# Last rows of a two-layer graph kernel: one-hot products and a sync-engine store in place of a GpSimd scatter

## The chip, the core and the metric

The kernel runs on one core of a Trainium2 chip. A core has TensorE (PE, matrix products), VectorE (DVE), ScalarE (ACT), GpSimd (POOL) and SyncE (SP), each with an instruction queue of its own; they meet through semaphores. Transfers are issued from a queue (SP's, ACT's or GpSimd's) and carried out by 16 DMA engines. The metric is the device time of one execution in microseconds (us), as the median of several runs.

## The reference

A graph of 6,250 nodes with 256 features and 106,250 edges sorted by destination (each node's last edge is its loop to itself), two layers. Cut to what matters:

```
S    = x[src]                                     # layer 0: a small net on each edge, by its type
msgs = where(rel == r, relu(relu(S @ W_r.T + b_r) @ W_r.T + b_r), msgs)      # r = 0, 1
agg  = segment_sum(msgs, dst)
x1   = layernorm(x + mlp(lstm_cell(agg)))

h    = x1 @ W                                     # layer 1: attention with 4 heads
e    = leaky_relu(a_src[src] + a_dst[dst])
ex   = exp(e - segment_max(e, dst)[dst])
y    = segment_sum(h[src] * ex, dst) / segment_sum(ex, dst) + bias + x1
out  = layernorm(x1 + relu(layernorm(y) * gamma + beta))                      # 6250 x 256, float32
```

Layer 1 in the kernel has the loop edges taken out of the list and added on their own.

## The kernel before

**Stages.** The front (gnn_kernel) computes layer 0's message rows for all nodes and both edge types on TensorE (`fph` L1228, `fpm` L1242, addition of the bias into `fms` on VectorE L1250, relu on ScalarE L1253, store to `parts` by SP L1255), while VectorE packs the edge list, GpSimd moves it by 21 indirect transfers (L944), and VectorE unpacks it into index tables. It ends with a flag `odd_i` (L1120 to L1125): if it is 0 all engines branch (L1281) into `fast`, else into a general kernel. The front's order is the planner's, helped by a few dependencies written by hand; `fast` runs under a manual schedule: each queue holds its instructions in the order in which the program emits them.

**Windows and groups.** The 100,000 list edges are 782 tiles of 128. Seven tiles are a window (NW = 112), and a window touches at most 64 consecutive destination rows, from `low[w]` on, a number that is known only on the chip. Two windows are a group (NG = 56): its 128 partitions are the 64 rows of its first window and the 64 of its second. For each tile GpSimd gathers 128 source rows (L1367, `G`), and TensorE adds them up with a one-hot matrix of slots (layer 0: L1777; layer 1: L2101, after VectorE's weighting in `weighted`, L1992).

**Layer 1.** At its start `complete` mends tiles that were gathered before the last rows of layer 0 were stored: VectorE builds one-hot matrices `ohS` from the loaded `srcb` and from `own_n` (L1853), TensorE multiplies (L1859). `own_n[p, q]` is the node that partition p of the q-th of the last LATE = 3 groups owns, or -1. When a group's sum is complete, `finish(g)` makes its 128 rows in the ring buffer `fy` (three of them): VectorE and ScalarE alternate, and the last step is ScalarE's normalisation (L2047). The rows of both windows are then stored by SP, each with 64 rows at `low[w]` (L2058). Neighbouring windows' stores overlap, so each waits until the one before it has landed. The windows of the last group are excepted (`lows_of` stops at NW - 2), because 64 rows from their start would go past the end of the result: group NG - 1 is scattered row by row by GpSimd, to the indices `tail_i` (L2060, where rows past the end are dropped). After it come the branch at the end of `fast` and, on every engine, the program's closing instructions (L2210).

Of the kernel before, what the change touches and what calls it, by code (L numbers as in the profile page):

```python
# [33 lines left out]
F32 = mybir.dt.float32  # L34
I32 = mybir.dt.int32
AF = mybir.ActivationFunctionType
OP = mybir.AluOpType
# [5 lines left out]
P = 128  # L43
N = 6250
D = 256
E = 106250
H = 4
# [20 lines left out]
NW = -(-TC // WT)  # L68
SLOTS = 64
NG = NW // 2  # L70
# [9 lines left out]
LATE = 3  # L80
# [627 lines left out]
def gnn_kernel(  # L708
# [26 lines left out]
    nc = tc.nc  # L735
# [4 lines left out]
    def rows(ap, n):  # L740
# [13 lines left out]
    iota_f = const.tile([P, P], F32, name="fiota")  # L754
    nc.gpsimd.iota(
        iota_f, pattern=[[1, P]], base=0, channel_multiplier=0, allow_small_or_imprecise_dtypes=True
# [16 lines left out]
    tail_i = const.tile([P, 1], I32, name="tail_i")  # L773
    tail_x = const.tile([P, 1], I32, name="tail_x")
    idx_e = const.tile([P, EARLY], I32, name="idx_e")
    own_n = const.tile([P, LATE], F32, name="own_n")


    with (
# [18 lines left out]
        with (  # L798
# [89 lines left out]
            moved = lp.tile([P, NC, HB + P], I32, name="moved")  # L888
# [53 lines left out]
            for k in range(NC):  # L942
                for b in range(3):
                    move = nc.gpsimd.indirect_dma_start(  # L944
                        out=packed,
                        out_offset=bass.IndirectOffsetOnAxis(ap=place[:CT, b, k : k + 1], axis=0),
                        in_=frame[:CT, k, b * HB : (b + 1) * HB],
                        in_offset=None,
# [62 lines left out]
            low = lp.tile([1, NW + 1], F32, name="low")  # L1011
            nc.vector.tensor_scalar(low, low_r, 1.0, None, op0=OP.add)
            nc.vector.memset(low[:, 0:1], 0.0)
            nc.vector.memset(low[:, NW:], float(N + 1))
            nc.vector.tensor_copy(low_i, low)
            wide = lp.tile([1, NW + 1], F32, name="wide")
            nc.vector.tensor_sub(wide[:, :NW], low[:, 1:], low[:, :NW])
            nc.vector.tensor_scalar(wide[:, :NW], wide[:, :NW], float(SLOTS), None, op0=OP.is_gt)
            nc.vector.tensor_scalar(
                wide[:, NW : NW + 1], low[:, NW - 3 : NW - 2], float(N - SLOTS), None, op0=OP.is_gt  # L1020
            )
            odd = lp.tile([1, 8], F32, name="odd")
            nc.vector.tensor_reduce(odd[:, 5:6], wide, axis=AX.X, op=OP.add)

            list_i = both[:CT, 0, :, :]
# [64 lines left out]
            for to, of in (  # L1090
# [31 lines left out]
            nc.vector.tensor_scalar(odd[:, 4:5], odd[:, 4:5], float(CT * NC - TC), None, op0=OP.subtract)  # L1122
            nc.vector.tensor_scalar(odd[:, 0:6], odd[:, 0:6], 0.0, None, op0=OP.not_equal)
            nc.vector.tensor_reduce(odd[:, 6:7], odd[:, 0:6], axis=AX.X, op=OP.add)
            nc.vector.tensor_scalar(odd_i, odd[:, 6:7], 1.0, None, op0=OP.min)  # L1125

            low_p = lps.tile([P, NW + 1], F32, name="low_p", bufs=1)
# [29 lines left out]
                op0=OP.is_ge,  # L1157
# [13 lines left out]
            for half, first_w, next_w in ((lo, w0, w0 + 1), (hi, w0 + 1, w0 + 2)):  # L1171
# [6 lines left out]
                    op0=OP.add,  # L1178
# [38 lines left out]
        for b0, bn in [(0, 1)] + [(1 + b, n) for b, n in blocks_of(NB - 1, CHUNK)]:  # L1217
# [6 lines left out]
            for r in range(2):  # L1224
                for m in range(2):
                    ph = mps.tile([P, CHUNK * P], F32, name="fph")
                    for k in range(2):
# [4 lines left out]
                            start=(k == 0),  # L1232
                            stop=(k == 1),
# [4 lines left out]
            for j in range(bn):  # L1238
                pm = mps.tile([P, 2, D], F32, name="fpm")
                for r in range(2):  # L1240
                    for k in range(2):
# [4 lines left out]
                            start=(k == 0),  # L1246
                            stop=(k == 1),
# [33 lines left out]
    with tc.If(odd_v == 0) as cmp:  # L1281
        fast(
            tc, x, WihT, bih, bhh, W1T, b1, W2T, b2, W3T, b3, Wg, att_src, att_dst, bias, gamma,
            beta, out, parts0, rows1, slots, cuts, kept, iota_f, iota_p, ident, idx0, idx1,
            first, mark, slot, low_i, tail_i, tail_x, idx_e, own_n, srcs,
        )
# [8 lines left out]
def fast(  # L1295
# [40 lines left out]
    nc = tc.nc  # L1336
# [12 lines left out]
    def windows_of(g):  # L1349
        return range(2 * g, 2 * g + 2)  # L1350

    def lows_of(ws):

        ws = [w for w in ws if w < NW - 2]
        return dict(zip(ws, lows(ws[0], len(ws)))) if ws else {}
# [18 lines left out]
    class Steps:  # L1374
# [18 lines left out]
        def finish(self):  # L1393
            while self.chains:
                self.step()

    def half_of(w):
        return slice(SLOTS * (w % 2), SLOTS * (w % 2 + 1))
# [42 lines left out]
    def ring(pool, shape, dtype, name, n):  # L1441

        of = rings.setdefault((name, id(pool)), [[], 0])
        if len(of[0]) < n:
            of[0].append(pool.tile(shape, dtype, name=f"{name}_{len(of[0])}"))
        of[1] += 1
        return of[0][(of[1] - 1) % n]
# [11 lines left out]
    def in_order(done, g):  # L1459
        if g != len(done):  # L1460
            raise ValueError("groups are out of order")
        done.append(g)
# [4 lines left out]
    with (  # L1467
# [320 lines left out]
        for n in range(TC + LAG):  # L1788
            if n < TC:
                g, t = order[n]  # L1790
# [21 lines left out]
            if n >= LAG:  # L1812
                g, t = order[n - LAG]
# [13 lines left out]
    with (  # L1827
# [171 lines left out]
        def finish(g, ps):  # L1999
            ws = windows_of(g)  # L2000
            u = everyone
            n = u.stop
            at_w = lows_of(ws)
            k3 = k3s[g]
            sm = ring(fp, [P, 4, H], F32, "sm", 3)
            w_own, den = sm[u, 0, :], sm[u, 1, :]
            nc.vector.tensor_sub(w_own, loop[u, g, :], ps[u, HA:])

            nc.vector.tensor_scalar(w_own, w_own, 0.0, None, op0=OP.min)
            nc.scalar.activation(w_own, w_own, AF.Exp)  # L2010
            yield 2

            nc.vector.tensor_scalar(w_own, w_own, 2.0, None, op0=OP.mult)
            nc.vector.scalar_tensor_tensor(
                den, ps[u, D:HA], 1e-16, w_own, op0=OP.add, op1=OP.add
            )
            nc.vector.reciprocal(den, den)
            yt = ring(fp, [P, D], F32, "fy", 3)
            y = yt[u, :]

            def heads(ap):
                return ap.rearrange("p (h f) -> p h f", h=H)

            nc.vector.tensor_mul(  # L2024
                heads(y), heads(k3[u, 2, :]), w_own[:, :, None].to_broadcast([n, H, F])
            )
            nc.vector.tensor_add(y, y, ps[u, :D])  # L2027
            read.add(g)
            yield 1
            nc.vector.tensor_mul(heads(y), heads(y), den[:, :, None].to_broadcast([n, H, F]))  # L2030
            nc.vector.tensor_add(y, y, k3[u, 1, :])  # L2031
            yield 1
            mv = ring(fp, [P, 2, 2], F32, "fmv1", 3)
            rs = ring(fp, [P, 2, 2], F32, "frs1", 3)

            def normed(k):
                st = ring(fp, [P, nc.vector.BN_STATS_DIM], F32, "fst1", 3)
                r, m = rs[u, k, 0:1], rs[u, k, 1:2]
                nc.vector.bn_stats(st[u, :], y)  # L2039
                nc.vector.bn_aggr(mv[u, k, :], st[u, :])  # L2040
                nc.scalar.activation(r, mv[u, k, 1:2], AF.Ln, bias=eps_c[u])  # L2041
                nc.scalar.activation(r, r, AF.Exp, scale=-0.5)
                yield 2
                nc.vector.scalar_tensor_tensor(  # L2044
                    m, mv[u, k, 0:1], -1.0, r, op0=OP.mult, op1=OP.mult
                )
                nc.scalar.activation(y, y, AF.Identity, bias=m, scale=r)  # L2047

            yield from normed(0)
            yield 2  # L2050
            nc.vector.tensor_mul(y, y, vec_p[u, 0, :])
            nc.vector.tensor_add(y, y, vec_p[u, 1, :])
            nc.vector.scalar_tensor_tensor(y, y, 0.0, k3[u, 0, :], op0=OP.max, op1=OP.add)
            yield 1
            yield from normed(1)
            in_order(written, g)
            for w in at_w:
                nc.sync.dma_start(out[bass.ds(at_w[w], SLOTS), :], yt[half_of(w), :])  # L2058
            if g == NG - 1:
                nc.gpsimd.indirect_dma_start(  # L2060
                    out=out,
                    out_offset=bass.IndirectOffsetOnAxis(ap=tail_i, axis=0),
                    in_=yt,
                    in_offset=None,
                    bounds_check=N - 1,
                    oob_is_err=False,
                )

        pair_of = {g: p for p in pairs for g in p}
        boxes = {p[0]: {} for p in pairs}  # L2070
        sums, queue, read, ohs, k3s, left, written = {}, [], set(), {}, {}, {}, []

        def sum1():

# [27 lines left out]
            if left[g] == 0:  # L2102
                run.start(finish(g, sums[g]), 1)

        def aheads():
            for pair in pairs:
                while run.now < 2 * WT * (pair[0] - (len(pair) == 1)):
                    yield 1
                yield from ahead(pair, boxes[pair[0]])

        run.start(aheads())
        t = 0
        while t < TC + LAG or late or queue or run.chains:
# [8 lines left out]
            if 0 <= k < TC:  # L2122
# [3 lines left out]
                g = w // 2  # L2126
# [87 lines left out]
```

## Time and profile before

| what | value |
|---|---|
| median of 3 runs | 2231.43 us (2231.18 to 2232.48) |
| the profiled execution | 2231.32 us, its span 2229.5 us, mean granted TensorE clock 0.829 |
| busy in the span | PE 1576.9, DVE 1259.0, ACT 506.4, POOL 1527.2 us |
| GpSimd gathers, both layers | 782 of 957 ns and 761 of 956 ns |
| first gather of layer 0, last gather of layer 1 | start at 196.91 us and 2177.11 us |
| last ScalarE instruction of group NG - 1 | 2216.27 us, 0.60 us long |
| the scatter of the last rows | 2217.15 us, 1.00 us long on GpSimd |

The span runs from the first to the last instruction on record. Busy time of GpSimd is the time in which it makes descriptors; the transfers themselves follow on the DMA engines. An engine's name with a q (SPq, POOLq) means its instruction sequencer: branches, waits and issues are recorded there and do not count as busy. In rows of a view by line, three durations are the minimum, median and maximum in ns.

### The profile page before, as it was taken

What the parts mean: (1) busy time and instruction counts of PE and PEld (TensorE: products, weight loads), DVE (VectorE), ACT (ScalarE), POOL (GpSimd) and SP (SyncE); (2) the same over time, 40 slices, a digit from 0 to 9 for tenths busy, and PEclk for the clock granted to TensorE, in tenths of its full rate; (3) what the DMA queues carried; (4) which work ended last, traced back from release to release, by engine and by line L of the source; (5) the groups of instructions that cost most, each with busy time, mean ns of one, the idle gap of its engine ahead of it and who ended that gap; (6) DMA issues with size and microseconds to landing.
All of it is one profiled execution on the core that took longest, in us unless ns stands there. A gap on an engine that the chain in (4) does not pass through costs nothing. (4 is left out here: it accounts for less than half of the span.)

```text
span 2229.5 us, 22334 instructions
## 1 busy us (share of the span) xinstructions
PE 1576.9 (71%) x5848; PEld 789.2 (35%) x5848; DVE 1259.0 (56%) x3374; ACT 506.4 (23%) x1526; POOL 1527.2 (68%) x1604
## 2 busy tenths in 40 slices
PE   8997788888888888888996754654545545454563
PEld 5664233333333333333453522322322223232331
DVE  7562134334333333333543688887777777777785
ACT  3332012221222212222343022212112111212121
POOL 1303777777777777777776777777777777777770
PEclk9998799899999899999997967766767677676776
DMA  5335435555455555554565556556555555555551
GB/s 165 131 103 155 130 114 172 165 153 149 147 171 165 146 151 155 170 168 134 178 175 162 150 145 165 156 145 165 148 153 156 144 159 143 164 155 145 156 151 38
DMA packets 163982, 334.33 MB, mean 150 GB/s; under 512 B 42538, under 2 KB 74398, under 8 KB 163845
## 3 DMA queue, kind: packets, MB, share of 16 engines
q0 software_dynamic: 75968, 208.00, 34.3%
q1 hardware_dynamic: 86085, 121.77, 17.3%
q10 hardware_dynamic: 1792, 3.05, 0.5%
q8 instruction: 48, 0.79, 0.1%
q14 instruction: 89, 0.73, 0.1%
HBM read 280.16 MB, written 52.53 MB: 149 GB/s over the span
## 5 line engine op out<-in xcount | busy, mean ns | idle before, releaser
L1367 POOL DMA_INDIRECT G<-parts,fidx x782 | 748.3, 957 | 330.5 <-issue 218.4
L1367 POOL DMA_INDIRECT G<-rows,fidx x761 | 727.4, 956 | 231.8 <-issue 214.2
L1777 PE MATMUL fps<-G,oh 128*64 128x257 f32 (+1 forms) x1674 | 528.1, 428 | 146.3 <-DMA G<-parts,fidx 129.5
L2101 PE MATMUL fps<-gw,oh 128*64 128x264 f32 (+1 forms) x1674 | 433.7, 463 | 246.3 <-DVE gw L1992 246.1
L2101 PEld LDWEIGHTS fps<-gw,oh 128*64 128x64 f32 (+1 forms) x1674 | 222.7, 164 | 411.9 <-DVE gw L1992 266.0
L1777 PEld LDWEIGHTS fps<-G,oh 128*64 128x64 f32 (+1 forms) x1674 | 193.6, 148 | 454.7 <-DMA G<-parts,fidx 237.2
L1992 DVE TENSOR_TENSOR gw<-G,bank 128x1792 f32<-128x1792 f32 (+1 forms) x167 | 248.9, 1490 | 62.4 <-ACT gw L1991 60.4
L1545 DVE TENSOR_SCALAR kind<-fps 128x1 f32<-128x1 f32 x112 | 12.5, 153 | 315.0 <-PE fps L1777 315.0
L1627 PE MATMUL fpg<-faT,fWihT 128*128 128x512 f32 (+2 forms) x432 | 170.9, 519 | 0.2 <-DVE faT L1563 0.2
L1452 DVE TENSOR_TENSOR oh<-bank,fslot 128x1024 f32<-128x1024 f32 x112 | 136.1, 1215 | 7.2 <-ACT bank L1971 7.2
L1940 PE MATMUL turn<-fident,e 128*120 128x128 f32 (+2 forms) x30 | 12.3, 412 | 155.3 <-ACT e L2136 155.3
L1242 PE MATMUL fpm<-fWrT,fhT 128*128 128x256 f32 x392 | 92.9, 392 | 5.3 <-DVE fms L1250 5.3
L1627 PEld LDWEIGHTS fpg<-faT,fWihT 128*128 128x128 f32 x432 | 70.9, 190 | 69.1 <-issue 59.4
L1738 DVE COPY nd<-hr 128x4 f32<-128x4 f32 x53 | 10.1, 190 | 149.7 <-ACT hr L1716 149.7
L1228 PE MATMUL fph<-fxc,fWrT 128*128 128x512 f32 (+1 forms) x208 | 88.8, 579 | 4.7 <-DMA fWrT<-in_WrT_dram 4.7
L2047 ACT ACTIVATE fy<-fy,frs 128x256 f32<-128x256 f32 x112 | 66.8, 596 | 86.9 <-DVE frs L2044 39.4
L2041 ACT ACTIVATE frs<-fmv,eps_c 128x1 f32<-128x1 f32 x112 | 32.9, 294 | 235.7 <-DVE gw L1986 152.7
L1242 PEld LDWEIGHTS fpm<-fWrT,fhT 128*128 128x128 f32 x392 | 75.6, 196 | 24.3 <-DVE fms L1250 9.1
L1710 PE MATMUL fpg<-Wx,fyT 128*128 128x264 f32 x224 | 74.2, 460 | 3.0 <-ACT fyT L1701 3.0
L944 POOL DMA_INDIRECT packed<-frame,place x21 | 20.9, 995 | 76.7 <-DVE frame L909 70.6
L1250 DVE TENSOR_TENSOR fms<-fpm,fbrr 128x512 f32<-128x512 f32 x49 | 33.6, 688 | 68.7 <-PE fpm L1242 62.8
L2144 ACT COPY e<-G 128x28 f32<-128x28 f32 x112 | 23.8, 213 | 183.8 <-DMA G<-rows,fidx 147.2
(253 smaller groups left out, 1863.4 us busy)
## 6 DMA issues: line engine op xcount, KB each, us to landing
kept<-keep SPq DMA_DIRECT2D x56, 384.0 KB
k<-kept SPq DMA_DIRECT2D x56, 384.0 KB
dB<-slots SPq DMA_DIRECT2D x112, 128.0 KB
loop<-parts SPq DMA_DIRECT2D x110, 128.0 KB
parts<-fms SPq DMA_DIRECT2D x49, 256.0 KB
G<-parts,fidx POOLq DMA_INDIRECT x782
G<-rows,fidx POOLq DMA_INDIRECT x761
fxn<-in_x_dram SPq DMA_DIRECT2D x110, 64.0 KB
```

What stands on the lines that cost most here:

```text
L1228: nc.tensor.matmul(ph[:, :cols], WrT_s[:, r, k, m * P : (m + 1) * P], xc[:, k, :cols], start=(k == 0), stop=(k == 1),)
L1242: made = nc.tensor.matmul(pm[:, r, :], hT[:, r, k, j * P : (j + 1) * P], WrT_s[:, r, k, :], start=(k == 0), stop=(k == 1),)
L1250: nc.vector.tensor_add(ms.rearrange("p r f -> p (r f)"), pm.rearrange("p r f -> p (r f)"), brr)
L1367: return nc.gpsimd.indirect_dma_start(out=to_tile, out_offset=None, in_=table, in_offset=bass.IndirectOffsetOnAxis(ap=idx, axis=0),)
L1452: nc.vector.tensor_tensor(to[:, :nj, :], iota_s[:, None, :].to_broadcast([P, nj, SLOTS]), of[:, :, None].to_broadcast([P, nj, SLOTS]), op= ...
L1627: nc.tensor.matmul(pg[:, :cols], WihT_s[:, k, c * P : (c + 1) * P], aT[:, k, :cols], start=(k == 0), stop=(k == 1),)
L1710: nc.tensor.matmul(ph[u, :], hs[i][:, k, u], Wx[:, k, :], start=(k == 0), stop=(k == 1))
L1777: nc.tensor.matmul(sums[g][to, :], ohj, got[t], start=begins, stop=ends)
L1992: nc.vector.tensor_mul(gw[:, :, :D].rearrange("p j (h f) -> p j h f", h=H), of[:, :n, :D].rearrange("p j (h f) -> p j h f", h=H), ex[:, o ...
L2041: nc.scalar.activation(r, mv[u, k, 1:2], AF.Ln, bias=eps_c[u])
L2047: nc.scalar.activation(y, y, AF.Identity, bias=m, scale=r)
L2101: nc.tensor.matmul(sums[g][to, :], ohj, gw, start=begins, stop=ends)
```

## The change

The last 128 rows of the result, 6122 to 6249, always lie in the last two groups if window NW - 4 begins at row 6122 or before. The changed kernel checks that on the chip (`odd[7]`, added into the flag), and builds at the start of layer 1 two one-hot matrices `shift[:, q, :]`: partition p of group NG - 2 + q goes to position `own_n - (N - 128)`. At the end, two products accumulate in PSUM the rows of both groups at their places, ScalarE copies them to a `fy` buffer, and SP stores them at the fixed address `out[N - 128 :]`. Group NG - 2 still has its own two stores before. The scatter by GpSimd is gone.

```
             nc.vector.tensor_copy(low_i, low)
+            odd = lp.tile([1, 8], F32, name="odd")
             wide = lp.tile([1, NW + 1], F32, name="wide")
+            nc.vector.tensor_scalar(
+                odd[:, 7:8], low[:, NW - 4 : NW - 3], float(N - P), None, op0=OP.is_gt
+            )
...
-            odd = lp.tile([1, 8], F32, name="odd")
...
             nc.vector.tensor_reduce(odd[:, 6:7], odd[:, 0:6], axis=AX.X, op=OP.add)
+            nc.vector.tensor_add(odd[:, 6:7], odd[:, 6:7], odd[:, 7:8])
...
                 nc.sync.dma_start(out[bass.ds(at_w[w], SLOTS), :], yt[half_of(w), :])
+            results[g] = yt
             if g == NG - 1:
-                nc.gpsimd.indirect_dma_start(
-                    out=out,
-                    out_offset=bass.IndirectOffsetOnAxis(ap=tail_i, axis=0),
-                    in_=yt,
-                    in_offset=None,
-                    bounds_check=N - 1,
-                    oob_is_err=False,
-                )
+                moved = ring(eps, [P, D + 2 * H], F32, "fps1", 2)[:, :D]
+                for q in range(2):
+                    nc.tensor.matmul(
+                        moved,
+                        shift[:, q, :],
+                        results[NG - 2 + q],
+                        start=(q == 0),
+                        stop=(q == 1),
+                    )
+                end = ring(fp, [P, D], F32, "fy", 3)
+                nc.scalar.copy(end, moved)
+                nc.sync.dma_start(out[N - P :, :], end)
...
+        results = {}
...
+        shift = ep.tile([P, 2, P], F32, name="shift")
+        own_q = ep.tile([P, 2], F32, name="own_q")
+        nc.vector.tensor_scalar(own_q, own_n[:, LATE - 2 :], float(N - P), None, op0=OP.subtract)
+        for q in range(2):
+            nc.vector.tensor_scalar(
+                shift[:, q, :], iota_f, own_q[:, q : q + 1], None, op0=OP.is_equal
+            )
         run.start(aheads())
```

## The prediction

> **What bounds the kernel now.** I read the page first: its costliest groups, then the chain that ended last. GpSimd's indirect gathers are the metronome.
>
> ```profile
> L1367 POOL DMA_INDIRECT G<-parts,fidx x782 | 748.3, 957 | 330.5 <-issue 218.4
> L1367 POOL DMA_INDIRECT G<-rows,fidx x761 | 727.4, 956 | 231.8 <-issue 214.2
> ```
>
> A gather takes 0.956 us and the next starts 0.30 us later. From the first at 196.91 us to the last at 2177.11 us the timeline shows one longer pause, 5.35 us at 1213.99. So what moves the first gather moves the end by as much, and what lies after the last gather (2177 to 2229.5) adds to the end directly. The chain of that tail, in order of time (start, us, what):
>
> ```profile
> 2209.03 0.50 ACT fy L2047
> 2209.54 1.92 DMA out_dram<-fy
> 2211.48 1.99 DMA out_dram<-fy
> ...
> 2213.76 3.15 issue
> ...
> 2217.15 1.00 POOL out_dram L2060
> ```
>
> The two stores of group NG-2 are serial and done at 2213.47. What releases GpSimd at 2217.15 is ScalarE's last normalisation, which by the timeline starts at 2216.27 and takes 0.60: the result is ready at 2216.87. From there to the span's end at 2229.5 are 12.6 us, though the scatter occupies GpSimd only to 2218.15. The instructions of the program's closing line and of the closing branch, in the last stretch (minimum/median/maximum ns, first and last start), tell the rest:
>
> ```profile
> L2210 SPq EVENT_SEMAPHORE  x14: 17/28/28, 2219.7 to 2229.5; - x14
> L2210 POOLq DRAIN  x3: 40/107/8880, 2219.8 to 2229.3; - x3
> L2210 SPq DRAIN  x3: 7/7/13, 2220.5 to 2229.0; - x3
> L2210 ACTq DRAIN  x2: 8/44/81, 2218.8 to 2229.0; - x2
> L2210 DVEq DRAIN  x2: 10/34/57, 2219.3 to 2229.0; - x2
> L1281 SPq COMPARE_BRANCH  x1: 38/38/38, 2212.0 to 2212.0; - x1
> L1281 DVEq COMPARE_BRANCH  x1: 51/51/51, 2216.2 to 2216.2; - x1
> L1281 ACTq COMPARE_BRANCH  x1: 38/38/38, 2216.3 to 2216.3; - x1
> L1281 POOLq COMPARE_BRANCH  x1: 41/41/41, 2216.9 to 2216.9; - x1
> ```
>
> The 8,880 ns can only be the first GpSimd DRAIN (2219.8 to 2228.7; from 2229.3 it would leave the span). The scatter has landed by 2219.7, where SP's wait on it ends, SP is done by 2220.6, and every other engine earlier. So 2220.6 to 2228.7 is GpSimd's DRAIN alone, and 0.8 us of closing barrier follow. Second reading: from branch to first closing instruction an engine needs 2.5 us (ACT), 2.9 (POOL), 3.1 (DVE); SP's own is hidden in its wait.
>
> **What the Trainium skill says.** "Runtime: NRT & Kernel Launch", section "Instruction fetch mechanics": a taken branch to a target outside the fetched pages stalls until a DMA brings that page. The 2.5 to 3.1 us agree. "VectorE: DVE Perf Modes", section "The DRAIN you can't avoid", calls the closing DRAINs on all engines about 12 ns; that fits SP (7 to 13 ns) and not GpSimd's 8,880 ns, and the trace decides. "DMA: Bandwidth & Descriptors", section "Anatomy of one DMA", puts some 2 us of fixed cost on a transfer, mostly the write's receipt; the stores' 1.92 and 1.99 us agree. "TensorE: Matmul & The Clock Gate", section "What's actually happening": the clock is half or full, set by activity in free-running windows of 3.41 us. The trace agrees (granted clock, by window: us, PE busy, PEld, DVE, ACT, POOL busy, PEclk, DMA):
>
> ```profile
> 137.90:141.31 3.41, 1.01 (x3) 0.19 (x1) 3.41 (x6) 0.02 (x1) 0.00 (x0) 1.00 0.00 0
> 141.31:144.72 3.41, 2.58 (x6) 2.14 (x7) 1.37 (x4) 1.72 (x3) 0.00 (x0) 0.50 0.22 80
> 144.72:148.13 3.41, 3.41 (x13) 2.51 (x12) 1.80 (x4) 0.63 (x1) 0.00 (x0) 0.50 0.22 80
> ```
>
> **The end, step by step.** Removed: the scatter on GpSimd, so its last instruction is the gather at 2177.11. Its branch, fetch and DRAIN then run from about 2178: 0.9 + 2.9 + 8.9 gives 2190, under the tail's work, which lasts 27 us longer. If the DRAIN is not of this kind, see the second rival. Added after 2216.87:
> - TensorE: the product with group NG-2 starts once that group is ready (2209.5) and is hidden. Its successor waits for the last group; nothing is queued behind it but the branch. 0.05 us for the signal (as DVE gw to PE at 2200.8). Its shape is that of the W3T product; TensorE will have idled over 6 us, so I take that product's instance at half clock:
>
> ```profile
> L1672 PE MATMUL fpg<-fW3T,fz x2: 634/716/797, 1178.2 to 1178.8; 128*128 128x256 f32 x2
> L1717 ACT COPY keep<-fpg x56: 378/378/385, 333.1 to 1213.6; 128x256 f32<-128x256 f32 x56
> ```
>
>   Start to end 1.22 us by the timeline (0.70 at full clock, the other bound).
> - ScalarE's copy out of PSUM: 0.03 + 0.38 us. Its ring buffers, group NG-3's, are free since about 2195.
> - SP's store: it waits on the copy and on the previous store, landed at 2213.47. Signal 0.02, issue 0.47 (each store's row), landing about 2.0 us after its start, 2.3 at most (the 384 KB kept<-keep store at 1214.01).
> - SP's branch and fetch: 0.05 + 2.8 (mean of the three engines; bounds 2.5 and the 3.47 of TensorE's branch record). The landing, some 1.5 us after the issue ends, is inside it. SP holds no work behind the store.
> - SP's twelve semaphore checks, 2219.7 to 2220.5: 0.84; the barrier 0.82.
>
> Sum: 0.05+1.22+0.03+0.38+0.02+0.47+0.05+2.8+0.84+0.82 = 6.7 us instead of 12.6, a gain of 5.9. With a free fetch the landing decides (gain 7.2); with 3.5 it is 5.2.
>
> **The front.** DVE gets one 1x1 comparison beside the window starts (0.13 us, as the `wide` one there) and one 1x1 addition before `odd_i` (0.15 us, the row of its neighbour). The first lies on the way to the fms addition at 141.41, for which TensorE waits: +0.13. The second ends before GpSimd needs anything: it waits until 196.9 for the last `parts` stores. Nothing. The built instruction order shows a side effect: the scheduler puts the first of two products of one `fph` (two records of 0.43 us) ahead of the wait in which TensorE idles 3.22 us (138.9 to 142.13). Its PSUM buffer is freed by a ScalarE relu finished at 137.9, so it runs there, and 0.86 us leave a stage in which TensorE sets the pace up to the last store. Net at the first gather: -0.7 (bounds: +0.3 if DVE soon binds, -4.2 with the first rival).
>
> **The middle.** own_q (0.17) and two comparisons of 128x128 (0.23 each, the `toward` row) come before `ohS`. They inherit its waits except that for `srcb`. DVE stands from 1214.9 to 1221.3 for srcb's load; the other condition, the kept store, is met at 1216.3, so the three end by 1217.2, hidden in that wait. Uncovered they would cost 0.6. Behind them stand only `ohS` and its followers, and no gather waits on those beyond its pitch of 0.30 us.
>
> Total -5.9 - 0.7 = -6.6 us. The profiled execution took 2231.32 us, 1.8 around its span of 2229.5: 2224.7; the median is 0.1 higher: **2224.8 us**. About 0.2% (4.5 us) is what a measurement of this kernel tells from no change.
>
> **Rivals.**
> 1. *The clock stays up at the front.* With 0.86 us more work, window 137.90:141.31 would be busy 1.87 of 3.41, 55%, instead of 30%. Comparing such windows over this trace, all but one of those that lost full clock were busy under 56%, and the lowest that kept it 44%: it is a toss, and the phase is free. Uncut, the 9.3 us of TensorE work from 142.13 to 151.5 halve, of which DVE's own work gives back a part: an estimated 3.5 us more, 2221.3.
> 2. *The DRAIN follows the program's last transfer, not GpSimd's.* It starts just after the scatter's landing, which speaks for it; that GpSimd waits for no semaphore there speaks against. Then: landing at 2220.6, + 8.9 + 0.8 = 2230.3, less 0.7, and 1.9 around: 2231.5, no change. The one-hot products then bought nothing.
> 3. *The tail is re-timed.* Shifted by 0.7 us against the clock windows, the last groups' products (half clock at 2186 to 2189 and 2200.8 to 2206.4) or the chain before the 1214 pause lose 2 to 4 us: 2227 to 2229, no change.
> 4. *Slower: TensorE's clock takes over in the first layer.* At 71% busy it has little spare; should the shift add half-clock windows (1.7 us lost in each) until it holds up G buffers, GpSimd slips. It decides from four lost windows exposed, and needs about seven to end 4.5 us above before: 2236. Against it: not one gather of the layer waits over 0.31 us.
>
> That the check added to `odd` sends everything to the general kernel is excluded: the last row bound is 6122, and with these inputs window NW-4 begins at row 6050.
>
> **How the numbers follow.** Likeliest case 58% (2224.8; its own range 2223.4 to 2226.6), rival 1 21% (2221.3), rival 2 7%, rival 3 10%, rival 4 4%. Faster by over 0.2% is the first two, 79%; within 0.2% rivals 2 and 3, 17%; slower 4%. The range 2220.0 to 2227.2 takes in the likeliest and most of rival 1, and leaves the others out.
>
> **What would show it.** Right: GpSimd's long DRAIN ends near 2190; the chain ends matmul, ACT copy, SP store; SP's first closing instruction comes 2.5 to 3.1 us after its branch; first gather near 196.2; span near 2223. Wrong: a GpSimd DRAIN of about 9 us after the last store (rival 2), full clock at 142 us (rival 1), a first gather later than before, or gathers that wait over 0.35 us (rival 4).

## The result and the profile after

| | before | after |
|---|---|---|
| median of 8 runs each | 2232.51 us (2229.69 to 2236.24) | 2224.31 us (2220.92 to 2227.55) |
| profiled execution, its span | 2231.32 us, 2229.5 us | 2222.75 us, 2221.0 us |
| first gather, last gather | 196.91, 2177.11 us | 194.18, 2172.79 us |
| last group ready | 2216.87 us | 2214.44 us |

The ratio of the runs is 0.9961, 95% interval 0.9952 to 0.9971: 8.7 us faster, 6.5 to 10.7. The prediction was 2224.8 us, a gain of 6.6.

Between the two profiled executions the span fell by 8.6 us: 6.1 at the end (from the last group to the span's end 12.67 us before, 6.52 after), 2.7 before the first gather, 1.6 between first and last gather, and 1.9 us were lost between the last gather and the last group. Only the first of these is wholly the change, as the runs below show. Seven of the twelve runs below took some 840 us longer, and so did the kernel before beside them (3071 or 3079 us); from these only the end and the last 55 us before the first gather are read, where their figures agree with those of the other runs.

The closing line of the program in the trace of after (last stretch; minimum/median/maximum ns, first and last start), to be read against the lines of L2210 before:

```profile
L2229 SPq EVENT_SEMAPHORE  x14: 17/28/28, 2219.3 to 2220.9; - x14
...
L2229 POOLq DRAIN  x3: 40/113/14176, 2168.5 to 2220.7; - x3
L2229 SPq DRAIN  x3: 7/7/13, 2220.1 to 2220.4; - x3
```

GpSimd's long DRAIN is still there, 14.2 us long now, but it starts at 2168.5 and ends at 2182.7, 38 us before the end. The closing branches, the same columns:

```profile
L1286 POOLq COMPARE_BRANCH  x1: 41/41/41, 2165.8 to 2165.8; - x1
...
L1286 SPq COMPARE_BRANCH  x1: 38/38/38, 2216.5 to 2216.5; - x1
```

GpSimd's sequencer branched at 2165.8, 7 us ahead of the start of its last gather: it hands gathers to the engine's queue and goes on. SP, which branched first of the engines shown before (2212.0), is now the last (2216.54). The chain that ended last shows what released it (start, us, what):

```profile
2213.84 0.61 ACT fy L2052
2214.45 0.04 issue
2214.49 1.24 PE fps L2068 x2
2215.75 0.37 ACT fy L2076
```

Normalisation, the last product at half clock, ScalarE's copy. Then SP issues the store at 2216.15, and its first closing instruction comes at 2219.30. The gathers, in the groups of the page, are as before to a nanosecond (mean of one: 957 and 956 ns before):

```profile
L1372 POOL DMA_INDIRECT G<-parts,fidx x782 | 747.8, 956 | 326.8 <-issue 217.2
L1372 POOL DMA_INDIRECT G<-rows,fidx x761 | 726.8, 955 | 231.8 <-issue 216.0
```

### The profile page after: what moved, and what is told of

Its sections match the earlier page's. It is cut to its first block, busy times and chain, and to the rows that moved or that the text cites. A ratio compares the mean times of both kernels' runs of the same rounds, so it can differ in the third digit from the quotient of the medians.

```text
span 2221.0 us, 22344 instructions
## 1 busy us (share of the span) xinstructions
PE 1576.4 (71%) x5852; PEld 790.4 (36%) x5852; DVE 1261.4 (57%) x3379; ACT 506.2 (23%) x1527; POOL 1524.8 (69%) x1603
```

## The experiments

Four questions were open: what GpSimd's DRAIN follows, what the front's new order is worth, when TensorE loses its full clock there, and what SP's closing work costs.

### What the DRAIN follows

Two kernels put something small back on GpSimd at the very end. The first, a copy of four columns with no transfer:

```
+                sm_last = fp.tile([P, 4], F32, name="sm_last")
                 nc.scalar.copy(end, moved)
                 nc.sync.dma_start(out[N - P :, :], end)
+                nc.gpsimd.tensor_copy(sm_last, end[:, 0:4])
```

> The changed kernel with one small copy on GpSimd (4 columns of the last tile to a scratch tile, no transfer) after ScalarE's copy, beside SP's store: GpSimd's last instruction is then as late as the scatter was. Theory A (GpSimd's closing DRAIN takes some 8.9 us after the last instruction of any kind): DRAIN about 8.9 us from some 2219, ends 2228, span about 7 us longer than the changed kernel's, 2230 to 2231. Theory B (it takes 8.9 us only after a transfer that GpSimd itself has made descriptors for; by 2216 that is long over): DRAIN under 0.2 us, GpSimd's branch and fetch (0.05 + 2.9 us) end with SP's, time within 0.5 us of the changed kernel's, 2224.5.

GpSimd's timeline after its last gather, and the closing line's DRAINs:

```profile
3069.48 0.18 POOL L2079 COPY sm_last<-fy 128x4 f32<-128x4 f32 x1 [76.77 <-ACT fy L2077]
```

```profile
L2231 POOLq DRAIN  x3: 40/107/8799, 3072.2 to 3081.6; - x3
```

GpSimd had been idle for 76.8 us, so that no transfer of its own was recent. Still the DRAIN took 8.80 us, from 3072.24, and the end came 14.13 us after the last group instead of 6.5. Theory A holds. In time the gain is gone: ratio to the kernel before 1.0003 (0.9985 to 1.0021). The second kernel gives GpSimd the final store, to a fixed address:

```
-                nc.sync.dma_start(out[N - P :, :], end)
+                nc.gpsimd.dma_start(out[N - P :, :], end)
```

> The changed kernel with its last store issued by GpSimd instead of SP: a plain transfer of 128 rows to a fixed address, with no indices. Theory (any transfer from GpSimd's queue leaves the long DRAIN): it is about 8.9 us again and starts after the branch's fetch near 2219, end from the last normalisation some 13.5 to 14.5 us, 2231 to 2233, no gain over before although the scatter is gone. Rival (only the indirect transfer, with its descriptors made from indices, leaves it): DRAIN under 0.2 us, 2224 to 2225.5 like the changed kernel.

```profile
3062.87 0.59 POOL L2077 DMA_DIRECT2D out_dram<-fy  x1 [77.41 <-ACT fy L2076]
```

```profile
L2229 POOLq DRAIN  x3: 40/113/8879, 3065.8 to 3075.3; - x3
```

8.88 us again, and 14.68 us from the last group to the end: 2.0 more than before the change, though nothing is scattered; the ratio to the kernel before is 1.0011 (0.998 to 1.0043). So the cost belongs neither to the scatter's indices nor to a transfer made last. GpSimd took it after each kind of last instruction that was tried (scatter, plain store, copy, gather), and the change gains because that instruction lies early. In all seven traces whose last store is on SP or ScalarE and whose GpSimd ends with its gathers, the DRAIN ended 8.74 us after the end of the last gather's descriptors (in after 2173.91 and, rounded, 2182.66), and began 4.2 to 4.9 us before that gather did. Every kernel here makes over 1,500 gathers on GpSimd; whether one without any has the long DRAIN too, no run shows.

### One part alone

The end without the new order in the front: against the changed kernel, the check of window NW - 4 is made late, in one fused instruction, and TensorE's order is that of before.

```
-            nc.vector.tensor_scalar(
-                odd[:, 7:8], low[:, NW - 4 : NW - 3], float(N - P), None, op0=OP.is_gt
-            )
...
-            nc.vector.tensor_add(odd[:, 6:7], odd[:, 6:7], odd[:, 7:8])
+            nc.vector.scalar_tensor_tensor(
+                odd[:, 6:7],
+                low[:, NW - 4 : NW - 3],
+                float(N - P),
+                odd[:, 6:7],
+                op0=OP.is_gt,
+                op1=OP.add,
+            )
```

> The late check once more, in undisturbed conditions: the end is new, the front's order on TensorE is that of the kernel before. Theory (end 6.0 to 6.2 us and order 0.6 us, the rest of the 8.7 us between the two kernels being the phase of the clock's windows): ratio to before 0.9965 to 0.9980, 2223 to 2225 us against 2229; from the 452nd record of TensorE to the first gather 55.3 us with one lost window, 58.0 with three; end 6.5 us. Rival (the order does nothing): ratio 0.9961 as for the changed kernel.

2219.73 us against 2228.75: ratio 0.9962 (0.9949 to 0.9975), a gain of 8.5 us (5.6 to 11.4); end 6.63 us. The ratio is that of the rival (0.9961) and just outside the theory's range, of which the interval covers most; its trace gave 55.20 us from that record to the first gather, where 55.3 was expected (table below).

The front alone: the kernel before with both instructions on `odd[7]`, scatter kept.

> The front alone once more, in undisturbed conditions (the kernel before with the two instructions on odd[7]; scatter kept). Theory: from the 452nd record of TensorE to the first gather 54.4 to 54.8 us with one lost window, 53.1 with none; ratio 0.998 to 0.9997. Rival: 1.000.

2227.14 us against 2228.75: ratio 0.9998 (0.9991 to 1.0004), a gain of 0.4 us, between a loss of 0.9 and a gain of 2.0 (the medians are 1.6 us apart). This too is nearer to the rival. The DRAIN was 8.88 us after the scatter, the end 12.43 us.

The changed kernel beside them:

> The changed kernel itself beside the two parts. If end and front add up, its gain is the sum of the late check's (about 6 us) and of the front's (0.6 us and up to some 2 us more by lost windows); ratio 0.9952 to 0.9971 as measured at first. From the 452nd record to the first gather 54.4 us with one lost window.

2222.93 us: ratio 0.9967 (0.9955 to 0.9980), 7.4 us (4.5 to 10.0). In time, then, the gain is the end's, and the front's is too small for these runs to tell from nothing. The traces give 6.1 us for the end and 0.6 for the order in the front (below); their sum, 6.7, lies inside the intervals of both comparisons of the changed kernel (6.5 to 10.7, 4.5 to 10.0). Whether anything of what the two ratios say beyond it, 2.0 and 0.7 us, is real, these runs don't resolve.

The same split was also run beside the kernel before at 3071 us (the end alone, the front alone) and at 3079 us (the late check, the front again). With the end alone and no check at all (the two instructions on `odd[7]` left out):

> The changed kernel without the two instructions on odd[7]: the comparison of window NW - 4 with row 6122 and its addition into the flag are left out, so the front is that of the kernel before and only the end is new. Theory (the gain is the end's 5.9 to 6.1 us, and the front's side effect is a gain of its own): end from the last normalisation to the span's end 6.5 us as in the changed kernel, first gather as in the kernel before at the same length of the half-clock stretch near 141 us (196.9 with three windows of 3.41 us), about 2225 to 2226 us, ratio to before 0.9973. Rival (the front gives nothing, all 8.2 us are the end's and the tail's): 2224, the same as the changed kernel, ratio 0.996. If the first gather moves although the front's order is that of before, its place is set by the clock's phase and not by the order.

With the late check:

> The changed kernel with its check of window NW - 4 as one fused instruction of VectorE late in the front, in place of the addition, so that the front's order on TensorE is that of the kernel before and the end is the new one. Theory (the product moved ahead of TensorE's wait is worth a gain of its own, 0.7 us and more where it shortens the half-clock stretch): first gather near 196.9 us with a stretch of three windows of 3.41 us, 2225 to 2227 us, ratio to before 0.9973 to 0.998. Rival (the order does nothing; the phase of the clock's windows against the program decides from one execution to the next): ratio 0.996 like the changed kernel, 2224.

And the front alone, twice:

> The kernel before with only the two instructions on odd[7] (and with them the product of fph that moves ahead of TensorE's wait near 139 us); the scatter by GpSimd stays. Theory: first gather 0.7 us earlier at an equal half-clock stretch, up to 4 us earlier where the stretch is one window shorter or more; the end still 12.6 us from the last normalisation, with GpSimd's DRAIN of 8.9 us after the scatter; 2231.5 us at the small end, 2228 to 2229.5 if the shorter stretch is usual, ratio 0.998 to 0.9997. Rival (the front's side effect is nothing but the phase of one execution): ratio 1.000, 2232.5, first gather spread as in the kernel before.

> The front alone once more (the kernel before with only the two instructions on odd[7]; scatter kept), for a ratio in undisturbed conditions. Theory: 2228 to 2231.8, ratio 0.998 to 0.9997, first gather at 196.2 or, with a shorter half-clock stretch, down to 193; GpSimd's DRAIN 8.9 us after the scatter, end 12.6 us. Rival: ratio 1.000, first gathers spread alike in both kernels.

Their ratios, each to the kernel before beside it: 0.9977 (0.9955 to 0.9999) for the end alone, 1.0009 (0.9987 to 1.0031) for the late check, 1.0005 (0.9978 to 1.0032) and 0.9996 (0.9978 to 1.0015) for the front. The late check missed its expectation here: its interval shows no gain of 0.2%. The runs of one kernel lie 33 to 61 us apart here, and the ratios do not settle the split; the two new ends were 6.70 and 6.59 us, the two old ones 12.49 and 12.41, as elsewhere.

### The front: order and clock, separated

The kernel before once more, for its trace alone:

> The kernel before once more, for its trace: how the half-clock stretch near 141 us falls in another execution. If the three lost windows of the first trace were the phase of that execution, this one has one (or two), and 55.2 to 55.5 us from the 452nd record of TensorE to the first gather instead of 58.0; if they belong to this order of the front, it is 58.0 again. End from the last normalisation 12.4 to 12.7 us, with GpSimd's DRAIN of 8.9 us.

Its windows around TensorE's wait (us; PE, PEld, DVE, ACT, POOL busy; granted clock, DMA share, GB/s):

```profile
139.53:142.94 3.41, 0.75 (x4) 0.68 (x5) 3.20 (x7) 0.78 (x2) 0.00 (x0) 1.00 0.00 0
142.94:146.35 3.41, 3.41 (x13) 2.85 (x11) 0.90 (x2) 1.22 (x3) 0.00 (x0) 0.50 0.42 153
146.35:149.77 3.42, 3.42 (x20) 2.82 (x19) 3.15 (x17) 0.36 (x1) 0.00 (x0) 1.00 0.22 85
```

It took 2229.33 us, another execution beside it 2227.64. The trace shows one window at half clock (a lost window, from here on), not the three (10.24 us) of the trace on which the prediction rested, and the first gather at 194.11 instead of 196.91. The long stretch was that execution's, not the kernel's. The trace of after has one window too:

```profile
140.69:144.10 3.41, 0.93 (x4) 0.85 (x5) 3.02 (x7) 0.95 (x2) 0.00 (x0) 1.00 0.00 0
144.10:147.51 3.41, 3.41 (x13) 2.57 (x12) 1.24 (x2) 1.38 (x3) 0.00 (x0) 0.50 0.43 159
```

And the front alone lost none in the run above:

```profile
138.94:142.35 3.41, 1.54 (x4) 0.38 (x2) 3.41 (x8) 0.00 (x0) 0.00 (x0) 1.00 0.00 0
142.35:145.77 3.42, 2.87 (x16) 2.46 (x17) 1.88 (x4) 1.78 (x4) 0.00 (x0) 1.00 0.22 78
```

The same wait, but the windows lie differently over it: 1.54 of 3.41 us busy, 45%, kept the clock; 0.93 (27%) and 0.75 (22%) lost it. Over all fourteen traces, eleven lost a window after one that was busy 4 to 31%, and the three that lost none had 45, 50 and 61%. To take the phase out I count from one fixed point, the end of TensorE's 452nd matmul record: the last before the wait in the old order, and the last before the moved records in the new. From there to the first gather:

| order on TensorE | lost windows | us to the first gather |
|---|---|---|
| as before | 3 | 58.00 (first trace of before) |
| as before | 1 | 55.25, 55.20, 55.44, 55.24 |
| one product ahead | 1 | 54.38, 54.77, 54.67, 54.73, 54.85, 54.62 |
| one product ahead | 0 | 53.04, 53.13 |

The means of the middle rows are 55.28 and 54.67: the order is worth 0.6 us. A lost window is worth 1.6 us (54.67 less 53.09), two further ones 2.7.

### SP's closing work, and a better version

SP's twelve checks follow its own branch and fetch only because SP makes the last store. Given to ScalarE:

```
-                nc.sync.dma_start(out[N - P :, :], end)
+                nc.scalar.dma_start(out[N - P :, :], end)
```

> The changed kernel with the last store issued by ScalarE, which made the copy, instead of SP. SP's branch, fetch and its twelve semaphore checks then come earlier except for those that need ScalarE's store, whose landing comes some 2.0 us after its issue. Theory (the path is the storing engine's branch and fetch of 2.5 to 2.8 us, and SP's checks of 0.84 us lie behind it only because SP itself stores): end from the last normalisation 5.5 to 6.0 us instead of 6.5, GpSimd's DRAIN hidden, about 2223.5. Rival (SP's checks are one chain behind the last landing, whoever stores): 6.3 to 6.6 us, no difference.

The closing line:

```profile
L2229 SPq EVENT_SEMAPHORE  x14: 17/28/1222, 3050.4 to 3058.3; - x14
L2229 POOLq DRAIN  x3: 40/113/14422, 2969.7 to 3058.1; - x3
...
L2229 ACTq DRAIN  x2: 8/44/80, 3057.5 to 3057.8; - x2
```

SP starts its checks at 3050.4, before the last group is ready (3052.71), and one of them then takes 1.2 us, which I read as its wait for the landing. The end came 5.67 us after the last group, as the theory said: 0.9 less than in the first trace of after (0.9 to 1.1 less over the other four with SP's store, 6.59 to 6.79 us). Its median is 3067.40 us beside 3079, ratio 0.9962 (0.9939 to 0.9986).

The last kernel adds two more things to this one: the product of group NG - 2 seven times over, so that TensorE is busy while it waits, and the second product of the `fph` tile ahead of the front's wait as well.

```
-                        nc.tensor.matmul(
+                        last = nc.tensor.matmul(
...
+                    if (b0, r, m) == (37, 1, 1):
+                        tc.add_manual_dep(
+                            ahead_of.ins, last.ins.name,
+                            mybir.DependencyInfo(
+                                mybir.DependencyClass.NoSync, mybir.DependencyReason.DATA
+                            ),
+                            reason="TensorE waits here",
+                        )
...
+                        if (b0 + j, r, k) == (35, 0, 0):
+                            ahead_of = made
...
-                for q in range(2):
+                for n, q in enumerate([0] * 6 + [0, 1]):
...
-                        stop=(q == 1),
+                        stop=(q == 1 or n < 6),
```

> A version meant to beat both kernels: the changed kernel with the last store on ScalarE, with the product of group NG - 2 by its matrix repeated six times ahead of the last product (the repeats overwrite each other, so that TensorE is busy while it waits), and in the front with the second product of the same fph tile also ordered ahead of TensorE's wait, by a dependency without a semaphore. Theory (each place is its own term): TensorE's wait near 140 us shrinks from 2.5 to about 1.65 us and no clock window is lost there, so that the time from the end of the 452nd record of TensorE (a matrix product of the front, the last before the wait in the kernel before) to the first gather falls from 54.4 us to 52.3 to 52.6; end from the last normalisation 5.1 to 5.2 us, with the last product at full clock (0.70 instead of 1.24 us); 2220 us in undisturbed conditions, ratio to before 0.9945. Rivals: the order in the front is worth nothing once no window is lost (53.1 us), or VectorE's own work after 143 us becomes the bound (53.5 us or more); the repeats do not bring the clock back in time (5.6 to 5.7 us).

2217.99 us against 2228.82: ratio 0.9955 (0.9941 to 0.9969), 10.0 us (6.9 to 13.2). TensorE's timeline at the front's wait and at the end:

```profile
134.10 7.03 PE L1233 MATMUL fph<-fxc,fWrT 128*128 128x512 f32 x16
142.74 1.99 PE L1256 MATMUL fpm<-fWrT,fhT 128*128 128x256 f32 x8 [1.60 <-DVE fms L1266]
...
2202.67 4.96 PE L2079 MATMUL fps<-fy,shift 128*128 128x256 f32 x14 [2.17 <-ACT fy L2063]
2209.79 0.70 PE L2079 MATMUL fps<-fy,shift 128*128 128x256 f32 x2 [2.15 <-ACT fy L2063]
```

The wait is 1.60 us, no window is lost, and the first gather comes 52.29 us after the fixed point; the last product takes 0.70 us instead of 1.24; the end is 5.29 us (0.1 more than expected). Term by term it gains, over the changed kernel, 2.4 us in the front (54.67 less 52.29; 0.8 of it against the traces that lost no window, the rest the window) and 1.2 at the end (6.52 less 5.29). The ratios of the two (0.9961 and 0.9967 against 0.9955) overlap, so that it is faster than the changed kernel rests on the terms of its one trace, not on the times. It beats the kernel before.

### What moves without the change

| trace | first to last gather | making descriptors | longest pause | last gather to last group | end |
|---|---|---|---|---|---|
| before, first | 1980.20 us | 1475.8 us | 5.35 us | 39.76 us | 12.67 us |
| before, again | 1980.60 | 1475.6 | 6.25 | 40.23 | 12.51 |
| front alone | 1978.08 | 1474.7 | 4.62 | 40.19 | 12.43 |
| late check | 1976.66 | 1472.3 | 5.76 | 39.80 | 6.63 |
| after, first | 1978.61 | 1474.6 | 5.36 | 41.64 | 6.52 |
| after, again | 1980.38 | 1476.4 | 5.35 | 41.84 | 6.79 |
| better version | 1976.71 | 1474.1 | 4.14 | 41.33 | 5.29 |

The second column is the sum of the 1,543 gathers' durations. It varies by 4.1 us from execution to execution (0.954 to 0.957 us for one), while their short pauses of 0.30 us add up to 469.1 or 469.2 us in all seven. The third is the one longer pause of GpSimd, between the layers (at 1213.99 us in the first trace of before), which ScalarE's `keep` ends; it varies by 2.1 us. These two make up nearly all of the middle's spread of 3.9 us, and neither goes by kernel: the changed kernel's middle is 1978.6 us once and 1980.4 once. So nothing shows the 1.6 us of the first pair of profiles to be an effect of the change; 1.2 of them are descriptors.

The fourth column falls into two groups, and the three longer tails are those of the kernels with both the new end and the new order. VectorE is behind in them already when the last gather starts: the same instruction (`fst<-fy`) begins 0.48 us before that start in each of the four shorter ones and 0.51 to 0.61 us after it in the three. TensorE's next products (`fps<-gw,oh`) therefore begin 8.93 to 8.94 us after the gather's start in the four, and 9.92 to 10.02 in the three. The clock adds to it. In the four, the window that ends 12.2 to 12.8 us after the gather's start is busy for 3.27 to 3.41 of 3.41 us and full clock follows; in the three, the window that ends 11.8 to 12.8 us after it is busy for only 1.90 to 2.77, and half clock lasts one window more. Why VectorE is behind is open: neither part of the change lies in that stretch, and seven traces do not rule out chance.

## Why the prediction was right

**The end (5.9 predicted, 6.1 in the first pair, 5.6 to 6.2 over all pairs of old and new ends in the table above).** Term by term in the first trace of after: signal 0.05 (0.05 predicted); product 1.24 at half clock (1.22); pause 0.02 and copy 0.37 (0.03 and 0.38); pause 0.03 and issue 0.34 (0.02 and 0.47); 0.05 to the branch and 2.76 from it to the first check (0.05 and 2.8); checks 0.84 (0.84); barrier 0.82 (0.82). In sum 6.52, against 6.7. The one term that was mis-sized is the issue: I took each window's store (0.47 us), whose address is known only on the chip, and the new one, at a fixed address, took 0.34; that the address makes the difference is likely but not tested apart. The landing was hidden in the fetch, as said.

**GpSimd's DRAIN.** It is hidden, as the step said, but the step's working put branch, fetch and DRAIN one after the other behind the last gather and came to 2190. The sequencer had branched and fetched while gathers were still queued, so the end was 2182.66, 8.74 us after the last gather's. Rival 2 (the DRAIN follows the program's last transfer) falls: the changed kernel's last transfer is SP's store at 2216.15, and the DRAIN had been over for 33 us. Nor is it the scatter's own: every last instruction of GpSimd that was tried has it.

**The front (0.7 predicted).** The step's net of 0.86 less 0.13 measured 0.6 at an equal number of lost windows, by the traces; the times do not resolve it. The predicted wait of TensorE, 3.22 less 0.86 plus 0.13, came out (2.51 us). What the prediction had not seen is that its own baseline, three lost windows, was one execution's: the second trace of before has one, so that a part of rival 1's gain is to be had in the old order too. The first gather came at 194.18, not near 196.2 as the prediction said. The 2.7 us by which the first gather came earlier in the first pair are 3.6 us of shorter way (0.6 of order, the rest two windows less) less 0.9 us by which that execution reached the fixed point later. Rival 1 gave 3.5 us for three windows; one costs 1.6. Its sign, full clock at 142 us, did appear in the trace of after, but only because the windows lay elsewhere: half clock came from 144.10 to 147.51. With the new order some executions lose none (two of eight traces) and with the old order none of five escaped, which fits a wait of 2.5 us instead of 3.3 under windows of 3.41, but so few traces don't make a rate.

**The middle (nothing predicted).** Confirmed: in the first trace of after the three new instructions of VectorE ran from 1213.05 to 1213.77 us, inside its wait for `srcb`, which lasted to 1217.27. The longest pause of the gathers, before them, was 5.35 us at 1213.99 before and 5.36 at 1210.48 after. No other gather waited over 0.31 us, so rival 4, the clock taking over, did not occur.

**Rival 3, the tail re-timed.** Something of its size occurred in both traces of the changed kernel: the tail was 1.4 to 2.1 us longer than in the two of the kernel before (the rival had 2 to 4), but not with the late check. A clock window lost for the last products is a part of it, as the rival had it; VectorE's lag of 1.0 us ahead of them is another, and its cause is open. It did not take the gain away.

**The sum.** 6.6 predicted; 8.7 (6.5 to 10.7) and 7.4 (4.5 to 10.0) measured. The terms that belong to the change come to 6.1 and 0.6, as the prediction had them, and for its reasons. That the first median is only 0.5 us below the forecast is partly luck. The kernel before was 1.1 us slower in these runs than in those on which the forecast was built (2232.51 and 2231.43). And in the profiled pair 2.0 us more than predicted came from the front, through windows that were the execution's, and 1.6 from the middle, while the tail took 1.9 back; the prediction had none of these.

## What to carry to other kernels

Look at what each engine does after its last instruction, not only at the last instruction: here GpSimd took 8.7 to 8.9 us to close, whichever of four kinds of instruction it had done last. By an estimate from these traces (8.9 us and up to 3.0 for branch and fetch) this is hidden where GpSimd ends some 12 us before the others have finished, while a four-column copy left at the end brings it all back. Look also at what closing work stands behind the engine that makes the last store: ScalarE instead of SyncE was worth 0.9 us here. And where a stage hangs on TensorE's clock, read several executions before a stretch at half clock is taken as the kernel's: the same kernel lost three windows in one and one in the next.

## What the runs showed of the hardware

- GpSimd's closing DRAIN of 8.80 us after a copy of 128x4, when its last gather's descriptors had ended 76.8 us before. The Trainium skill, "VectorE: DVE Perf Modes", section "The DRAIN you can't avoid", calls the closing DRAINs of all engines about 12 ns constant; SP's 7 to 13 ns agree, GpSimd's in no run here does.
- After the front's wait TensorE mostly had its clock back at the end of one window, busy 2.98 to 3.41 us. In the first trace of before it took three, though the second, 144.72 to 148.13, was busy throughout, and the third as well. The Trainium skill, "TensorE: Matmul & The Clock Gate", section "What's actually happening", has the clock back after one busy window or more, which both agree with. Why it took longer there is not known.
